# Spreading B, C and the time step over the partitions: transfers through DRAM in place of products with ones and zeros

## The chip, the core and the metric

The kernel runs on one core of one Trainium2 chip. Its engines work side by side, each through its own list of instructions in order: TensorE (PE, products; its weight loads are listed as PEld), VectorE (DVE), ScalarE (ACT), GpSimd (POOL) and SyncE (SP), which here only issues transfers. An engine waits for another through semaphores. The metric is the device time in microseconds (us), as the median of several executions.

## The reference

One layer for 8 sequences ("batches") of 512 steps and 512 channels: a layer norm, a selective scan (Mamba) on 1024 inner channels with 16 states each, a gated feed-forward network whose gate is modulated by an attention, and `x + s * silu(g)`. What the change touches is the part of the scan that comes from a projection on 33 columns:

```python
p = x_conv @ W_x.T                       # 33 columns
Bm, Cm = p[..., :16], p[..., 16:32]
dt = softplus(p[..., -1] + mean(dt_bias))
A = -exp(A_log)
def step(h, inp):
    x_t, B_t, C_t, dt_t = inp
    h = exp(A * dt_t) * h + dt_t * B_t * x_t
    y_t = einsum('bds,bs->bd', h, C_t)
```

All of it is in 32-bit floats.

## The kernel before

**Two stages.** The attention of all batches comes first (to about 760 us of the span), and writes its results to DRAM. Then a long loop goes over 8 batches x 64 scan steps. A scan step holds 8 channels x 16 states on the 128 partitions, for two groups of channels, with the 512 time steps along a row. Scan step k is split in two "chunks", one for each group. For each group ACT makes the decay `exp(A dt)` (line 549), DVE runs the scan instruction (569); the input is multiplied by dt B on DVE or POOL in turn (561, 563), and the result by C on POOL (574). After four scan steps PE sums over the states with a 0/1 matrix (`y`, 586), three scan steps later than the last of the four.

**What runs in the gaps.** All large products are cut into parts of about four matmuls, in one list for each batch (`batch_parts`): the gate and up products of the feed-forward net (293), its down products (`down_proj`, 355), the output products of the batch before (384), the input products and convolutions of the batch after (201, `conv_in`), the z gates, and the step sizes of the batch after (`step_size`). The main loop runs parts in proportion to the scan steps done. A part returns follow-up work with a delay in chunks: `(1, copies)` runs one chunk after the part. So the order on each engine is written out by the program, and no engine reorders it.

**Loads.** `prefetch` looks up to eight parts ahead and loads weights, in SP's queue: at most three quarters of a down product are ahead of the one in use (four buffers, `wd`). The scan inputs `x` are loaded five scan steps ahead (`load_scan`, eleven buffers), each 512 KB, repeated over 16 partitions. SP issues in program order; a load that has to wait for its buffer holds all behind it.

**B, C and dt before.** For batch b+1, `step_size` works during batch b's down products, in five parts placed between quarters of the products for m = 0, 1, 2. `project` makes the 33 rows `p`, in two halves (rows 0 to 32 and 64 to 96) that ACT copies to `parts_p`. `turned` turns the last row into a column with four small products; DVE and ACT compute softplus on 128 x 4. `step` spreads dt: DVE builds a diagonal `dg`, PE multiplies it by ones, ACT copies the result (`dt`). `output` and `input_` spread C and B with the 0/1 matrix `lift`, which also adds the two halves; ACT copies C (`cc`), DVE multiplies B by dt (`bb`). The scan of batch b+1 uses `dt` in its decays, `bb` in its inputs and `cc` in its outputs.

The attention stage has a spread through DRAM of its own: for batches 1 to 7 `statistics` writes 512 numbers to `scr_r` in the same turned way and reads them back as a row for all partitions (`rms`, lines 856 and 857).

Of the kernel before, what the change touches and what calls it, by code (L numbers as in the profile page):

```python
# [10 lines left out]
F32 = mybir.dt.float32  # L11
AF = mybir.ActivationFunctionType
ALU = mybir.AluOpType
# [4 lines left out]
P = 128  # L18
NB = 8
S = 512  # L20
DM = 512
KT = DM // P
TT = S // P
DI = 1024
ND = DI // P
NS = 16
# [13 lines left out]
def mamba_gated_ffn_kernel(  # L40
# [22 lines left out]
    nc = tc.nc  # L63

    const = ctx.enter_context(tc.tile_pool(name="const", bufs=1))
    dram = ctx.enter_context(tc.tile_pool(name="scratch", bufs=1, space=DRAM))

    scr_x = [dram.tile([P, 2 * KT, S], F32, tag=f"scr_x{b}", name=f"scr_x{b}") for b in range(NB)]
    scr_m = [dram.tile([R, S], F32, tag=f"scr_m{b}", name=f"scr_m{b}") for b in range(NB)]
    scr_c = [dram.tile([DI, S], F32, tag=f"scr_c{b}", name=f"scr_c{b}") for b in range(NB)]  # L70
    scr_r = [dram.tile([S], F32, tag=f"scr_r{b}", name=f"scr_r{b}") for b in range(NB)]
# [10 lines left out]
    act = ctx.enter_context(tc.tile_pool(name="act", bufs=2))  # L82
    xcp = ctx.enter_context(tc.tile_pool(name="xcp", bufs=2 * ND))
    tmc = ctx.enter_context(tc.tile_pool(name="tmc", bufs=2))
# [7 lines left out]
    def bank(name):  # L92
        if banks["special"]:
            return banks["special"](name)
        banks["n"] += 1
        pool = banks["second"] if banks["second"] and banks["n"] % 4 // 2 else ps_1
        return pool.tile([P, 512], F32, tag="mm", name=name)
# [3 lines left out]
    def load_xn(b):  # L101
        xnt[b] = act.tile([P, KT, S], F32, tag="xnt", name=f"xnt_{b}")
        nc.sync.dma_start(xnt[b], scr_x[b][:, :KT, :])

    def load_h(b):
        ht[b] = act.tile([P, KT, S], F32, tag="ht", name=f"ht_{b}", bufs=1)
        nc.sync.dma_start(ht[b], scr_x[b][:, KT:, :])
        modh[b] = act.tile([4 * QD, S], F32, tag="modh", name=f"modh_{b}", bufs=1)
        for i in range(4):
            nc.sync.dma_start(modh[b][i * QD : i * QD + R, :], scr_m[b])  # L110

    xc, gates, mlp, modh, spread, ys = {}, {}, {}, {}, {}, {}
# [14 lines left out]
    parts_p = wp.tile([P, S], F32, tag="parts_p", name="parts_p")  # L127
# [293 lines left out]
    def step_size(b):  # L421

        st = {}
        W = 2 * NS + 1

        def project():

            ps = bank(f"ps_p_{b}")
            for d in range(ND):
                at = 64 * (d % 2)  # L430
                nc.tensor.matmul(  # L431
                    ps[at : at + W, :], lhsT=wx[:, d, :], rhs=xc[b, d], start=(d < 2),
                    stop=(d >= ND - 2),
                )

            def copies():
                for at in (0, 64):
                    nc.scalar.copy(parts_p[at : at + W, :], ps[at : at + W, :])
                st["parts"] = parts_p

            return [(1, copies)]

        def lifted(i, name):
            ps = bank(f"ps_{name}_{b}")
            nc.tensor.matmul(ps, lhsT=lift[:, i, :], rhs=parts_p, start=True, stop=True)
            return ps

        def turned():

            ps = bank(f"ps_v_{b}")  # L450
            for tt in range(TT):
                nc.tensor.matmul(
                    ps[:, tt : tt + 1], lhsT=st["parts"][:, ts(tt, P)], rhs=lift[:, 2, 0:1],
                    start=True, stop=True,
                )
            st["v"] = ps[:, :TT]
            return [(1, exponential), (2, logarithm), (3, softplus)]

        def exponential():
            s = tmc.tile([P, 5, TT], F32, tag="sp", name=f"sp_{b}")
            st["sp"] = v, ee, ww, ln, dd = [s[:, i, :] for i in range(5)]
            nc.vector.tensor_scalar(v, st["v"], mb, None, ALU.add)
            nc.scalar.activation(ww, v, AF.Abs)
            nc.scalar.activation(ee, ww, AF.Exp, scale=-1.0)

        def logarithm():
            v, ee, ww, ln, dd = st["sp"]
            nc.vector.tensor_scalar(ww, ee, 1.0, None, ALU.add)  # L470
            nc.scalar.activation(ln, ww, AF.Ln)
            nc.vector.tensor_scalar(dd, ww, 1.0, None, ALU.subtract)
            nc.vector.tensor_scalar(ww, dd, 0.0, None, ALU.is_equal)
            nc.vector.tensor_tensor(dd, dd, ww, ALU.add)
            nc.vector.reciprocal(dd, dd)
            nc.vector.tensor_tensor(dd, dd, ee, ALU.mult)

        def softplus():
            v, ee, ww, ln, dd = st["sp"]
            nc.vector.tensor_tensor(ln, ln, ww, ALU.add)  # L480
            nc.vector.tensor_tensor(ln, ln, dd, ALU.mult)
            nc.vector.scalar_tensor_tensor(dd, v, 0.0, ln, ALU.max, ALU.add)
            dg = tmc.tile([P, TT, P], F32, tag="conv", name=f"dg_{b}")
            nc.vector.tensor_tensor(
                dg, ident.unsqueeze(1).to_broadcast([P, TT, P]),
                dd.unsqueeze(2).to_broadcast([P, TT, P]), ALU.mult,
            )
            st["dg"] = dg

        def step():  # L490
            ps = bank(f"ps_dt_{b}")
            nc.tensor.matmul(
                ps, lhsT=ones, rhs=st["dg"].rearrange("p t c -> p (t c)"), start=True, stop=True
            )
            st["sd"] = act.tile([P, S], F32, tag="dt", name=f"dt_{b}")
            nc.scalar.copy(st["sd"], ps)
            return []

        def output():
            ps = lifted(1, "cc")  # L500
            sc = act.tile([P, S], F32, tag="cc", name=f"cc_{b}")
            nc.scalar.copy(sc, ps)
            st["sc"] = sc
            return []

        def input_():
            ps = lifted(0, "bb")
            sb = act.tile([P, S], F32, tag="bb", name=f"bb_{b}")

            def scaled():  # L510
                nc.vector.tensor_tensor(sb, ps, st["sd"], ALU.mult)
                spread[b] = (sb, st["sc"], st["sd"])

            return [(1, scaled)]

        return (
            [(4, [], project)], [(1, [], turned)], [(1, [], step)], [(1, [], output)],
            [(1, [], input_)],
        )

# [80 lines left out]
    def batch_parts(b):  # L601

        quads = [gate_up(b, fq) for fq in range(NF // 4)]
        sizes = ([], [], [], [], [])
        parts = quads[0][0] + quads[0][1]
        if 0 < b < NB - 1:
            parts.insert(1, (0, [], lambda: load_xn(b + 1)))
        convs = [[]] * ND
        if b + 1 < NB:
            convs = [conv_in(b + 1, d) for d in range(ND)]  # L610
            sizes = step_size(b + 1)
        if b > 0:
            done = [finish(b - 1, m) for m in range(KT)]
            parts += done[0][0] + done[1][0] + [done[0][1]] + done[2][0] + [done[1][1]]
            parts += convs[0] + done[3][0] + [done[2][1]] + convs[1]
            turns = [done[3][1]]
        else:
            parts += convs[0] + convs[1]
            turns = []
        parts += quads[1][0] + turns + convs[2] + quads[1][1] + convs[3] + convs[4]  # L620
        parts += quads[2][0] + convs[5] + quads[2][1] + convs[6]
        parts += quads[3][0] + convs[7] + quads[3][1]
        for m in range(KT):
            down = down_proj(b, m)
            if m == 0:
                parts += down[:2] + sizes[0] + down[2:3] + sizes[1] + down[3:]
            elif m == 1:
                parts += down + sizes[2]
            elif m == 2:
                parts += down[:1] + sizes[3] + down[1:2] + sizes[4] + down[2:]  # L630
            else:
                parts += down
            if m == 0 and b + 1 < NB:
                parts.append((0, [], lambda: load_h(b + 1)))
        total = sum(p[0] for p in parts) + 4 * ND
        done, out_, z = 0, [], 0
        for p in parts:
            while z < ND and done >= total * (8 * z + 5) / STEPS and not p[3:]:
                out_ += z_gate(b, z)
                done += 4  # L640
                z += 1
            out_.append(p)
            done += p[0]
        while z < ND:
            out_ += z_gate(b, z)
            z += 1
        return out_
# [38 lines left out]
    with ExitStack() as c1:  # L686
# [423 lines left out]
        sizes = step_size(0)  # L1110
# [34 lines left out]
        for g in range(len(items)):  # L1145
# [3 lines left out]
            b, hg = cur  # L1149
# [18 lines left out]
            convs = g - (len(items) - 5)  # L1168
# [13 lines left out]
            for s in range(TT):  # L1182
                for w in ORDER[s]:
# [23 lines left out]
                    elif todo[w]:  # L1207
                        f = todo[w].pop(0)
# [70 lines left out]
    for b in range(NB):  # L1279
# [3 lines left out]
        for s in range(STEPS):  # L1283
            k = b * STEPS + s
            if s == STEPS - 6 and b + 1 < NB:

                parts = batch_parts(b + 1)
# [100 lines left out]
```

## Time and profile before

| | |
|---|---|
| median of 3 runs | 3105.28 us (3104.54 to 3106.17) |
| the profiled execution | 3103.03 us, its span 3101.2 us |
| granted TensorE clock, mean | 0.995 |
| attention stage, 0 to 760 us: PE busy | 715.66 us |
| 1330 to 1530 us: PE, DVE, ACT, POOL busy | 200.00, 176.00, 78.84, 155.59 us |
| transfers in that stretch | 209 GB/s, DMA share 0.78 |
| bytes moved in all | 505.10 MB |

The span is the time from the first to the last instruction of one execution that the hardware profiler recorded; the execution's own time is a little more. "Busy" counts the time in which an engine works on at least one instruction. A row of the timeline has the start, the length, the engine, the line of the kernel, the operation, the tile written and the tiles read, the shape and the number of instructions; in brackets stands how long the engine had been idle before and which instruction ended that. The waits of SP are those of its transfers' issues, not of the transfers.

### The profile page before, as it was taken

What the parts mean: (1) busy time and instruction counts of PE and PEld (TensorE: products, weight loads), DVE (VectorE), ACT (ScalarE), POOL (GpSimd) and SP (SyncE); (2) the same over time, 40 slices, a digit from 0 to 9 for tenths busy, and PEclk for the clock granted to TensorE, in tenths of its full rate; (3) what the DMA queues carried; (4) which work ended last, traced back from release to release, by engine and by line L of the source; (5) the groups of instructions that cost most, each with busy time, mean ns of one, the idle gap of its engine ahead of it and who ended that gap; (6) DMA issues with size and microseconds to landing.
All of it is one profiled execution on the core that took longest, in us unless ns stands there. A gap on an engine that the chain in (4) does not pass through costs nothing.

```text
span 3101.2 us, 34502 instructions
## 1 busy us (share of the span) xinstructions
PE 3046.4 (98%) x11740; PEld 1358.7 (44%) x11740; DVE 2611.0 (84%) x3393; ACT 1332.3 (43%) x2248; POOL 1902.8 (61%) x876
## 2 busy tenths in 40 slices
PE   8999999988999999999999999999999999999999
PEld 4555555544433444444344434444444444444443
DVE  6888888865999889879987988898889878988885
ACT  4555656544444334433443433344334433443332
POOL 3111111100788877777777777777777777778884
PEclk9999999999999999999999999999999999999999
DMA  3111111111977787678677867877787778777874
GB/s 115 46 46 46 45 45 46 59 46 47 236 209 190 193 226 203 181 200 218 187 200 200 225 175 206 216 203 183 193 227 193 191 191 224 201 187 187 218 198 114
DMA packets 295263, 505.10 MB, mean 163 GB/s; under 512 B 30352, under 2 KB 161936, under 8 KB 290480
## 3 DMA queue, kind: packets, MB, share of 16 engines
q1 hardware_dynamic: 293680, 494.25, 59.9%
q0 software_dynamic: 1408, 8.65, 0.7%
q8 instruction: 94, 1.54, 0.2%
q14 instruction: 81, 0.66, 0.1%
HBM read 460.53 MB, written 42.29 MB: 162 GB/s over the span
## 4 chain that ended last, share of the span: by engine, by line
PE 92%; DVE 5%; issue 1%; DMA 1%; ACT 1%; POOL 0%; SPq 0%; POOLq 0%; ACTq 0%; DVEq 0%
PE ps_gu L293 28%; PE ps_acc L355 14%; PE ps_in L201 14%; PE y L586 8%; PE ps_out L384 7%; PE ps_pt L1012 4%; PE ps_k L966 3%; PE ps_q L966 3%; PE s L981 3%; PE o_ps L1026 2%; PE ps_z L948 2%; PE ps_gu L304 1%; DVE x L569 1%; PE ps_p L431 1%; DVE mx L991 1%
## 5 line engine op out<-in xcount | busy, mean ns | idle before, releaser
L574 POOL TENSOR_TENSOR x<-x,cc 128x1024 f32<-128x1024 f32 x512 | 1203.9, 2361 | 500.5 <-DVE x L569 471.4
L569 DVE TENSOR_TENSOR_SCAN x<-decay,x 128x512 f32<-128x512 f32 x1024 | 1206.4, 1209 | 31.2 <-ACT decay L549 31.2
L549 ACT ACTIVATE decay<-dt,an 128x511 f32<-128x511 f32 x1024 | 695.8, 687 | 653.9 <-DVE x L569 649.2
L293 PE MATMUL ps_gu<-ht,wgu 128*128 128x512 f32 x2048 | 910.8, 597 | 0.8 <-DVE mod_t L1063 0.8
L293 PEld LDWEIGHTS ps_gu<-ht,wgu 128*128 128x128 f32 x2048 | 381.4, 190 | 517.9 <-issue 473.6
L563 POOL TENSOR_TENSOR x<-x,bb 128x1024 f32<-128x1024 f32 x256 | 605.0, 2363 | 4.2 <-DMA x<-scr_c 4.2
L201 PE MATMUL ps_in<-xnt,win 128*128 128x512 f32 x1024 | 459.8, 595 | 1.2 <-DVE m L323 1.2
L355 PE MATMUL ps_acc<-m,wd 128*128 128x512 f32 x1024 | 453.9, 596 | 0.0
L1064 POOL DMA_DIRECT2D scr_m<-mod_t x8 | 4.0, 498 | 577.1 <-DVE mod_t L1063 505.9
L561 DVE TENSOR_TENSOR x<-x,dtb_ps 128x1024 f32<-128x1024 f32 x256 | 306.2, 1196 | 3.7 <-DMA x<-scr_c 2.6
L355 PEld LDWEIGHTS ps_acc<-m,wd 128*128 128x128 f32 x1024 | 191.2, 190 | 253.8 <-issue 247.3
L201 PEld LDWEIGHTS ps_in<-xnt,win 128*128 128x128 f32 x1024 | 191.0, 190 | 244.7 <-issue 222.8
L997 ACT ACTIVATE p<-s,mx 128x384 f32<-128x384 f32 (+3 forms) x512 | 238.0, 525 | 133.5 <-DVE mx L991 129.9
L586 PE MATMUL y<-x,sel 128*32 128x512 f32 x2048 | 252.9, 601 | 3.7 <-POOL x L574 3.6
L384 PE MATMUL ps_out<-xc,wout 128*128 128x512 f32 x512 | 225.9, 594 | 0.0
L991 DVE TENSOR_REDUCE mx<-s 128x2 f32<-128x256 f32 (+3 forms) x256 | 211.1, 825 | 8.8
L240 DVE SCALAR_TENSOR_TENSOR conv<-ps_in,cw,conv 128x511 f32<-128x511 f32 (+2 forms) x192 | 143.5, 747 | 66.1 <-ACT conv L259 61.5
L1012 PE MATMUL ps_pt<-ident,p 128*128 128x128 f32 x1280 | 181.7, 279 | 12.6 <-DVE xc L250 5.8
L1012 PEld LDWEIGHTS ps_pt<-ident,p 128*128 128x128 f32 x1280 | 141.8, 141 | 92.8 <-issue 46.1
L384 PEld LDWEIGHTS ps_out<-xc,wout 128*128 128x128 f32 x512 | 95.8, 190 | 121.4 <-issue 121.4
L1017 DVE COPY pt<-ps_pt 128x512 f32<-128x512 f32 x191 | 123.3, 682 | 26.0 <-PE ps_pt L1012 25.1
L987 DVE TENSOR_TENSOR s<-s,mask 128x256 f32<-128x256 f32 x256 | 109.1, 426 | 36.9 <-PE s L981 36.0
(182 smaller groups left out, 2244.8 us busy)
## 6 DMA issues: line engine op xcount, KB each, us to landing
x<-scr_c SPq DMA_DIRECT2D x512, 512.0 KB
wgu<-in_w_ffn SPq DMA_DIRECT2D x256, 256.0 KB
win<-in_w_in SPq DMA_DIRECT2D x128, 256.0 KB
wd<-in_w_ffn SPq DMA_DIRECT2D x128, 256.0 KB
scr_c<-xc SPq DMA_DIRECT2D x64, 256.0 KB
wout<-in_out_w SPq DMA_DIRECT2D x64, 256.0 KB
xt<-in_x SPq DMA_DIRECT2D x32, 256.0 KB
scr_x<-xnT SPq DMA_DIRECT2D x8, 1024.0 KB
```

What stands on the lines that cost most here:

```text
L201: nc.tensor.matmul(ps, lhsT=w[:, kt, :], rhs=xnt[b][:, kt, :], start=(kt == 0), stop=(kt == KT - 1))
L293: nc.tensor.matmul(st[i, which], lhsT=w[:, kt, :], rhs=ht[b][:, kt, :], start=(kt == 0), stop=(kt == KT - 1 and (which == 1 or i == 3)),)
L355: nc.tensor.matmul(st["acc"], lhsT=w[:, j, :], rhs=mlp[b, f], start=(f == 0), stop=(f == NF - 1))
L384: nc.tensor.matmul(st["ps"], lhsT=w[:, d % 4, :], rhs=xc[b, d], start=(d == 0), stop=(d == ND - 1),)
L549: nc.scalar.activation(decay[n][:, 1:], spread[b][2][:, 1:], AF.Exp, scale=an[:, g // 4, g % 4 : g % 4 + 1])
L561: nc.vector.tensor_tensor(t, t, dtb_ps.unsqueeze(1).to_broadcast([P, 2, S]), ALU.mult)
L563: nc.gpsimd.tensor_tensor(t, t, spread[b][0].unsqueeze(1).to_broadcast([P, 2, S]), ALU.mult)
L569: nc.vector.tensor_tensor_scan(t, decay[n], t, 0.0, ALU.mult, ALU.add)
L574: nc.gpsimd.tensor_tensor(t, t, spread[b][1].unsqueeze(1).to_broadcast([P, 2, S]), ALU.mult)
L586: nc.tensor.matmul(y[ts(j, QD), :], lhsT=sel[:, i0 + n, :], rhs=xs[k - 3 + j][:, n, :], start=(i0 + n == 0), stop=(i0 + n == 3),)
L991: nc.vector.reduce_max(mx[i], sc[i][:, :, :w], axis=AX.X, negate=True)
L1012: nc.tensor.transpose(ps[:, ts(h, P)], probs[b, hg, qt][:, h, ts(kt, P)], ident)
```

## The change

For the first batch nothing changes, except that its steps are described by the same functions. For the other seven, `project` is the only part left on PE. ACT copies the upper half of `p`, DVE adds the lower one to it, and SP writes the 33 rows to a new tile in DRAM, `scr_p`. Two chunks later SP reads the last row back as a column (`v`) and B and C as rows, each repeated on 8 partitions. Softplus is as before, at chunks 7 to 9 after the part; its result goes to the last row of `scr_p` as single elements, and two chunks on (`rows`, 11) comes back as a row for all 128 partitions. At chunk 14 DVE multiplies B by dt. In `batch_parts` the five places for step sizes become one: ahead of all down products, after the last gate and up products; convolution 7 moves up by one place so that `project` has all it needs.

```diff
+    scr_p = [
+        dram.tile([2 * NS + 1, S], F32, tag=f"scr_p{b}", name=f"scr_p{b}") for b in range(NB)
+    ]
...
-            return [(1, copies)]
+            if b == 0:
+                return [(1, copies)]
+
+
+            def copy():
+                nc.scalar.copy(parts_p[64 : 64 + W, :], ps[64 : 64 + W, :])
+
+            def add():
+                nc.vector.tensor_tensor(parts_p[:W, :], ps[:W, :], parts_p[64 : 64 + W, :], ALU.add)
+
+            def send():
+                nc.sync.dma_start(scr_p[b], parts_p[:W, :])
+
+            def spread_out():
+                st["v"] = tmc.tile([P, TT], F32, tag="v", name=f"v_{b}", bufs=1)
+                nc.sync.dma_start(st["v"], scr_p[b][2 * NS].rearrange("(t p) -> p t", p=P))
+                st["sc"] = act.tile([P, S], F32, tag="cc", name=f"cc_{b}")
+                st["sb"] = act.tile([P, S], F32, tag="bb", name=f"bb_{b}")
+                for i, t in enumerate((st["sb"], st["sc"])):
+                    r = scr_p[b][i * NS : (i + 1) * NS, :]
+                    nc.sync.dma_start(t, r.unsqueeze(1).to_broadcast([NS, P // NS, S]))
+
+            return [
+                (1, copy), (2, add), (2, send), (4, spread_out), (7, exponential), (8, logarithm),
+                (9, softplus),
+                (11, rows), (14, scaled),
+            ]
...
             nc.vector.scalar_tensor_tensor(dd, v, 0.0, ln, ALU.max, ALU.add)
+            if b:
+                nc.sync.dma_start(scr_p[b][2 * NS].rearrange("(t p) -> p t", p=P), dd)
+                return
...
+        def rows():
+            st["sd"] = act.tile([P, S], F32, tag="dt", name=f"dt_{b}")
+            nc.sync.dma_start(st["sd"], scr_p[b][2 * NS].partition_broadcast(P))
+
+        def scaled():
+            nc.vector.tensor_tensor(st["sb"], st["sb"], st["sd"], ALU.mult)
+            spread[b] = (st["sb"], st["sc"], st["sd"])
...
+        if b:
+            return ([(4, [], project)],)
...
-        sizes = ([], [], [], [], [])
+        sizes = ([],)
...
-        parts += quads[2][0] + convs[5] + quads[2][1] + convs[6]
-        parts += quads[3][0] + convs[7] + quads[3][1]
+        parts += quads[2][0] + convs[5] + quads[2][1] + convs[6] + convs[7]
+        parts += quads[3][0] + quads[3][1] + sizes[0]
         for m in range(KT):
             down = down_proj(b, m)
-            if m == 0:
-                parts += down[:2] + sizes[0] + down[2:3] + sizes[1] + down[3:]
-            elif m == 1:
-                parts += down + sizes[2]
-            elif m == 2:
-                parts += down[:1] + sizes[3] + down[1:2] + sizes[4] + down[2:]
-            else:
-                parts += down
+            parts += down
             if m == 0 and b + 1 < NB:
                 parts.append((0, [], lambda: load_h(b + 1)))
```

More of the change, by code (lines that the diff above doesn't have):

```diff
@@ L508, in input_, with multiplied @@
             sb = act.tile([P, S], F32, tag="bb", name=f"bb_{b}")
-            def scaled():
+            def multiplied():
                 nc.vector.tensor_tensor(sb, ps, st["sd"], ALU.mult)
                 spread[b] = (sb, st["sc"], st["sd"])
-            return [(1, scaled)]
+            return [(1, multiplied)]
+        if b:
+            return ([(4, [], project)],)
         return (
```

## The prediction

> **What bounds the kernel now.** I read the page's busy shares first, then busy time by stage, then the order of work round one batch's step sizes, then who waits on whom.
>
> ```profile
> PE 3046.4 (98%) x11740; PEld 1358.7 (44%) x11740; DVE 2611.0 (84%) x3393; ACT 1332.3 (43%) x2248; POOL 1902.8 (61%) x876
> ```
>
> TensorE is busy for all but 2% of the span. By stage (stretch, its length, then PE, PEld, DVE, ACT, POOL busy, granted clock, DMA share, GB/s) it is sharper:
>
> ```profile
> 950.00:1030.00 80.00, 76.44 (x241) 29.90 (x234) 71.42 (x77) 33.53 (x52) 66.72 (x30) 0.98 0.75 190
> 1030.00:1250.00 220.00, 220.00 (x681) 90.02 (x680) 193.21 (x210) 87.12 (x137) 169.24 (x73) 1.00 0.78 207
> 1530.00:1630.00 100.00, 100.00 (x304) 41.00 (x303) 81.83 (x90) 39.00 (x61) 74.56 (x33) 1.00 0.71 188
> ```
>
> After the first batch of the scan PE never stops: batches repeat every 294.0 us (`ps_p` starts at 1559.0, 1853.1, 2147.1, 2441.1 and 2735.2). What leaves PE there is gained in full, and what makes PE wait there is lost in full. DVE, 82 to 88% busy in these rows, has slack but feeds PE: scan (DVE), then product with C (POOL), then `y` (PE).
>
> **What goes from PE.** One batch's steps on PE (start, length, instructions; a logical 512-column product is two instructions):
>
> ```profile
> 1559.04 3.63 PE L431 MATMUL ps_p<-xc,wx 128*33 128x512 f32 x16
> ...
> 1568.08 1.05 PE L452 MATMUL ps_v<-lift,parts_p 128*128 128x1 f32 x8
> 1568.99 10.55 PE L355 MATMUL ps_acc<-m,wd 128*128 128x512 f32 x24
> ...
> 1591.73 1.02 PE L492 MATMUL ps_dt<-dg,ones 128*128 128x512 f32 x2
> 1592.59 3.60 PE L355 MATMUL ps_acc<-m,wd 128*128 128x512 f32 x8
> 1596.02 1.02 PE L445 MATMUL ps_cc<-parts_p,lift 128*128 128x512 f32 x2
> 1596.88 3.60 PE L355 MATMUL ps_acc<-m,wd 128*128 128x512 f32 x8
> 1600.31 1.02 PE L445 MATMUL ps_bb<-parts_p,lift 128*128 128x512 f32 x2
> 1601.26 1.92 PE L586 MATMUL y<-x,sel 128*32 128x512 f32 x16
> ```
>
> From each start to the next: `ps_v` 0.91, `ps_dt` 0.86, `ps_cc` 0.86, `ps_bb` 0.95: 3.58 us a batch, on the engine that sets the end. Seven batches: **-25 us**. `ps_p` (3.55) stays.
>
> **What else moves, at nothing.** ACT loses three copies a batch (0.58 + 0.58 + 0.59); at 43% busy it is not the bound. DVE swaps the `dg` product (0.69) for the addition of the two halves of `ps_p` (as the nearest row, `bb` from PSUM, 0.69). The wait of DVE and ACT for `ps_p` stays, since the one copy left still waits for it. The bank of `ps_p` is held a chunk longer, which four banks cover; four fewer banks per batch leave their rotation as it was. New traffic is about 0.84 MB a batch, against 200 GB/s times 294 us = 59 MB: 1.4%, under a DMA share of 0.7 to 0.8. conv 7 moves ahead of the last gate products, on the same engines.
>
> **What is added: a chain through SP's queue.** SP issues in order and its loads wait for PE to free buffers, so it stands about where PE stands. I lay the changed order of batch 4 (2 to 7 are alike) on PE's own durations: T = 0 where `ps_p` starts, 3.43 for a quarter `d` of a down product, 3.52 for a z product, 1.86 for a burst of `y`. PE: `ps_p` to 3.6, d0.0 and d0.1 to 10.4, `y` to 12.3, d0.2 to d1.1 to 26.0, z to 29.5, `y` to 31.4, d1.2 to d2.1 to 45.1, then the `y` of the scan steps 244 to 247.
>
> 1. Copy (0.58) and addition end near T+5. SP has waited at `send` since before T; behind it stands d0.3's weight load, which PE needs at 15.7: hidden. `send` is whole 2 KB rows; it lands by about 8, then v, bb, cc are issued. They land by about 13 to 15, DVE wants v at 16.4 (242's scans, the `y` it waits for at 12.3, one product): no wait.
> 2. The softplus keeps its length:
>
> ```profile
> 1571.93 0.22 DVE L464 TENSOR_SCALAR sp<-ps_v,mb 128x4 f32<-128x4 f32 x1
> ...
> 1578.99 2.22 DVE L482 SCALAR_TENSOR_TENSOR sp<-sp 128x4 f32<-128x4 f32 x1
> ```
>
> 1571.93 to 1581.21 is 9.3, so the time step is ready at T+25.7. SP waits for it from about 16.7; behind it stand `ht`, `modh` and the loads of d1.3 (needed at 34.8) and d2.0 (38.2).
>
> 3. The time step is written to DRAM as 512 separate 4-byte elements and read back as a row for 128 partitions. The kernel has the same pair already, `scr_r` and `rms` in the attention stage:
>
> ```profile
> 496.30 0.38 SPq L856 DMA_DIRECT2D scr_r<-rs  x1
> 505.05 0.32 SPq L857 DMA_DIRECT2D rms<-scr_r  x1
> ```
> ```profile
> 511.07 1.27 POOL L939 TENSOR_TENSOR hT<-xnT,rms 128x512 f32<-128x512 f32 x1 [1.99 <-DMA rms<-scr_r]
> ```
>
> SP waited 8.75 us here for 2 KB to land, and 10.2 at 247.3; over the seven the mean is 9.1. From the read's issue to POOL's start: 4.1 to 6.5, mean 5.6. So dt lands at 25.8 + 9.1 + 0.5 (a weight issue between) + 5.6 + 0.8 (estimate: 256 KB of weights ahead of it, and the 1 MB of `ht`, which went out just before) = **T+41.8**.
>
> 4. DVE reaches `scaled` at about T+34 (eight rows after softplus, 1.13 a scan) and stands still for 8 us; every scan stands behind it. Then `scaled` and 246's second scan, POOL's product of 246 (2.36), its input product of 249 (2.36), its product of 247 (2.36): the `y` of 244 to 247 is ready 9.0 after dt, at T+50.8. PE wants it at 45.1. **PE waits 5.7 us.** Meanwhile d2.0 and d2.1 are loaded late too, since the order of the changed program lets SP issue d2.0 only after the element write has landed (it takes that write's semaphore, eight transfers on): d2.0 lands near 38.5 for 38.2, d2.1 behind 1.3 MB near 43.6 for 41.7. Both fit inside the same 5.7.
>
> Sum per batch: -3.6 + 5.7 = +2.1; seven batches +15. In the first stretch above PE already loses 3.56 us once, at batch 1's sizes; that wait is replaced, not added to: **+11 us**. The profiled run took 3103.03 (span 3101.2): 3114. The median of the runs is 2.25 above it: 3116.
>
> **A rule against the row.** The Trainium skill, "DMA: Bandwidth & Descriptors", section "Anatomy of one DMA — SWDGE (gpsimd) path", gives a transfer a fixed cost of about 2.0 us plus its bytes over 436 GB/s. By it 2 KB takes 2.0 and 256 KB 2.6, dt lands at 25.8 + 2.0 + 0.5 + 2.6 = T+31, before DVE asks, and the whole 25 us are kept: 3080. The same page ("Rules for kernel authors") warns that a last dimension that isn't contiguous becomes one descriptor per element, and ("Specifications") that under 512 B a transfer reads, modifies and writes; that speaks against this change, and the 8.75 us row is on its side. I take the row.
>
> **Bounds.** By the rows' ends (8.5 + 4.1, without the 0.8; 10.2 + 6.5 with it) PE waits 2.8 to 7.7 a batch; times seven, less 25 and less the 3.56 of batch 1, that is -9 to +25 us: 3096 to 3130. The rows come from a stage with DMA nearly idle; here it is at 0.7 to 1.06, so the upper end is nearer.
>
> **Rivals.**
> - *The transfers are hidden* (the rule's time, or DVE far enough ahead of PE): 3080, or up to 3099 where PE waits less than 3.2 a batch. For it: DVE waits for PE often (3.99 us at `ps_p`), so it has room. Against: the 8.75 us row, and only some 2 us between the unstalled `y` (T+43) and PE.
> - *Break-even*: PE waits 3.2 to 5.0 a batch, about what it is spared: 3099 to 3111. For it: the shorter rows give this. Against: they come from an idle DMA.
> - *SP's holds starve PE of weights*. Place: d1.3 and d2.0, with three quarters (10.3 us) of cover. SP stands 9 us at the softplus, then up to 9 for the write. From a landing of 12 us on, d2.0 lands near 42, then d2.1 behind the row and two 512 KB loads near 47, and the `y` near 54: a wait of 9, 9 x 7 - 25 - 3.6 = +34: 3139 or more. For it: 1 MB of `ht` sits in the same place. Against: loads there take 3 to 9 us in the trace and none stalled PE.
> - *It doesn't do what it says*: batch 0 keeps its products in either version; nothing else stays.
>
> **Chances.** Late time step with a wait of 5.0 to 8, 0.48; hidden, wholly or mostly, 0.25; break-even 0.15; starved weights 0.12. A change under 0.2% (6 us) can't be told from none. So faster 0.25, same 0.15, slower 0.60. Range 3080 to 3138, which takes in the hidden case and leaves out the starved one; the likeliest case alone is 3111 to 3132.
>
> **What would show it.** Right: PE busy falls by 25 us, yet gaps of 4 to 8 us appear on PE before a `y`, once a batch, some 45 us after `ps_p`, released by POOL; DVE idles at `scaled` for the dt row; SP waits about 9 us for the element write. Wrong: no such gaps and batches of 290.4 us (hidden), or gaps at L355's weights (starved). If the element write lands in 2 us here, or DVE comes to `scaled` later than T+40, the forecast fails to the fast side.

## The result, and the profile after

The changed kernel takes 3150.32 us (median of 4 runs, 3148.23 to 3151.93), the kernel before 3105.33: a ratio of 1.0147, 95% interval 1.0134 to 1.0159. It is slower by 45 us, four times the 11 us that were forecast and outside the range. The profiled execution has a span of 3149.5 us, against 3101.2.

The first row of the page shows TensorE with less work, in a longer span.

```profile
PE 3041.6 (97%) x11642; PEld 1350.9 (43%) x11642; DVE 2616.6 (83%) x3393; ACT 1320.1 (42%) x2227; POOL 1904.8 (60%) x876
```

PE is busy only 4.8 us less than before, although 98 instructions and 25 us of work are gone: where PE runs, it runs slower in places (below). Its idle time, span less busy time, has grown by 53.1 us, from 54.8 to 107.9. The page's rows for the down products, before and after (busy time, mean ns, idle time just before them), say where:

```profile
L355 PE MATMUL ps_acc<-m,wd 128*128 128x512 f32 x1024 | 453.9, 596 | 0.0
...
L358 PE MATMUL ps_acc<-m,wd 128*128 128x512 f32 x1024 | 469.0, 613 | 52.5 <-DMA wd<-in_w_ffn 52.5
```

Batches now repeat every 301 to 302 us (`ps_p` starts at 1262.3, 1563.8, 1865.1, 2167.4, 2468.2 and 2769.0) in place of 294.0.

Who waits for whom, in the changed kernel (us in total, times, longest):

```profile
DVE bb L527 <- DMA dt<-scr_p: 93.8, 7, 15.1
...
PEld ps_acc L358 <- DMA wd<-in_w_ffn: 63.7, 14, 8.9
...
PE ps_acc L358 <- DMA wd<-in_w_ffn: 52.5, 12, 8.1
...
PEld y L628 <- POOL x L616: 22.2, 23, 2.9
```

PE waits for the weights of the down products, which never held it in the kernel before. For `y` it waits no more than before (there 30.7 us, 36 times). DVE's wait for dt is long, 13.4 us a time, but it isn't what ends PE's waits: the 52.5 us for weights are all but the whole growth of PE's idle time.

One batch on PE, by time (start, length, instructions; in brackets the idle time before and what ended it); the first row is from the kernel before, two quarters at full speed:

```profile
1552.08 7.03 PE L355 MATMUL ps_acc<-m,wd 128*128 128x512 f32 x16
...
1865.11 3.63 PE L434 MATMUL ps_p<-xc,wx 128*33 128x512 f32 x16
...
1896.80 3.70 PE L358 MATMUL ps_acc<-m,wd 128*128 128x512 f32 x8
1908.31 9.71 PE L358 MATMUL ps_acc<-m,wd 128*128 128x512 f32 x16 [7.81 <-DMA wd<-in_w_ffn]
1918.90 3.70 PE L358 MATMUL ps_acc<-m,wd 128*128 128x512 f32 x8 [0.88 <-DMA wd<-in_w_ffn]
```

PE stands still at d1.3 for 7.8 us, then takes 9.7 for two quarters, which took 7.03 before, then waits once more, for d2.1. What happened to those weights is in SP's own queue:

```profile
1890.51 0.37 SPq L513 DMA_DIRECT2D scr_p<-sp  x1
1890.92 0.50 SPq L110 DMA_DIRECT2D ht<-scr_x  x1
1891.51 1.77 SPq L113 DMA_DIRECT2D modh<-scr_m  x4
1893.38 0.39 SPq L226 DMA_DIRECT2D wd<-in_w_ffn  x1
1893.87 0.53 SPq L583 DMA_DIRECT2D x<-scr_c  x1
1902.19 0.39 SPq L226 DMA_DIRECT2D wd<-in_w_ffn  x1
1905.43 0.34 SPq L524 DMA_DIRECT2D dt<-scr_p  x1
```

The element write goes out at 1890.51. The load for d1.3 is issued at 1893.38 and PE can use it at 1908.31, 14.9 us later. SP itself stands still too: it issues d2.0 only at 1902.19, when the write has landed, and the read of dt only at 1905.43, when `ht` has. Over the run:

```profile
SPq L226 <- DMA scr_p<-sp: 34.7, 6, 7.7
SPq L524 <- DMA ht<-scr_x: 27.4, 6, 5.9
```

And in the stretches of 2 us from there (the last three columns are granted clock, DMA share and GB/s):

```profile
1892.00:1894.00 2.00, 2.00 (x7) 0.80 (x6) 2.00 (x3) 1.33 (x2) 0.60 (x1) 1.00 2.56 66
1894.00:1896.00 2.00, 2.00 (x15) 0.60 (x17) 2.00 (x3) 1.00 (x3) 2.00 (x2) 1.00 0.51 33
1896.00:1898.00 2.00, 2.00 (x13) 0.68 (x4) 2.00 (x3) 0.99 (x2) 2.00 (x1) 1.00 1.07 33
1898.00:1900.00 2.00, 2.00 (x6) 0.76 (x4) 0.40 (x1) 0.69 (x1) 2.00 (x2) 1.00 0.66 25
1900.00:1902.00 2.00, 0.50 (x2) 0.00 (x0) 0.00 (x0) 0.00 (x0) 0.42 (x1) 1.00 0.28 25
1902.00:1904.00 2.00, 0.00 (x0) 0.00 (x0) 0.00 (x0) 0.00 (x0) 0.00 (x0) 0.82 0.82 297
1904.00:1906.00 2.00, 0.00 (x0) 0.00 (x0) 0.00 (x0) 0.00 (x0) 0.00 (x0) 0.50 1.06 273
...
1908.00:1910.00 2.00, 1.69 (x2) 0.84 (x3) 0.00 (x0) 0.00 (x0) 0.00 (x0) 0.50 1.15 198
```

For ten microseconds behind the write, with 1 MB of `ht` and more in the queue, the 16 DMA engines together move 25 to 66 GB/s, then at once 297. The DMA share is no help in seeing it here: it counts the time that packets took, and they took long. The bytes show it. At the end of the wait PE's granted clock is at 0.50, which is where the 9.71 us come from.

So the theory to test: **W**, the write of 512 single elements holds up the transfers behind it for some 10 us, and PE runs out of weights. Its rivals: **H**, SP standing at the softplus is enough, since it delays the same loads; **B**, the 1 MB of `ht` ahead of the weights is the cause; **D**, DVE's wait for dt is.

### The profile page after: what moved, and what is told of

It is laid out like the page before. It is cut to its first block, busy times and chain, and to the rows that moved or that the text cites. A ratio compares the mean times of both kernels' runs of the same rounds, so it can differ in the third digit from the quotient of the medians.

```text
span 3149.5 us, 34332 instructions
## 1 busy us (share of the span) xinstructions
PE 3041.6 (97%) x11642; PEld 1350.9 (43%) x11642; DVE 2616.6 (83%) x3393; ACT 1320.1 (42%) x2227; POOL 1904.8 (60%) x876
## 4 chain that ended last, share of the span: by engine, by line
PE 83%; DVE 7%; DMA 5%; issue 2%; POOL 2%; ACT 1%; SPq 0%; POOLq 0%; ACTq 0%; DVEq 0%
PE ps_gu L296 27%; PE ps_in L204 12%; PE ps_acc L358 9%; PE ps_out L387 7%; PE y L628 7%; PE ps_pt L1047 4%; PE ps_k L1001 3%; PE ps_q L1001 3%; PE s L1016 3%; PE o_ps L1061 2%; DMA wd<-in_w_ffn 2%; DMA ht<-scr_x 2%; PE ps_z L983 2%; DVE x L611 1%; POOL x L616 1%
## 5 line engine op out<-in xcount | busy, mean ns | idle before, releaser
L358 PE MATMUL ps_acc<-m,wd 128*128 128x512 f32 x1024 | 469.0, 613 | 52.5 <-DMA wd<-in_w_ffn 52.5
```

The costliest lines, as they stand in the source:

```text
L358: nc.tensor.matmul(st["acc"], lhsT=w[:, j, :], rhs=mlp[b, f], start=(f == 0), stop=(f == NF - 1))
```

## Experiments

Each was run beside the kernel before; that took 3103.97 with e1 to e4, 3105.29 with e5 to e8, 3103.2 with e9 to e11. e7 and e8 have four runs each, the others one.

### e1: no element write

```diff
-                nc.sync.dma_start(scr_p[b][2 * NS].rearrange("(t p) -> p t", p=P), dd)
                 return
...
-            nc.sync.dma_start(st["sd"], scr_p[b][2 * NS].partition_broadcast(P))
+            nc.sync.dma_start(st["sd"], scr_r[b].partition_broadcast(P))
```

> The element write is left out, and the row of dt comes from the 512 numbers that the attention stage left in DRAM (so dt is not the time step; B and C are as before). All else, the row's transfer at chunk 11 too, stays. Theory W (the write of 512 single elements holds up the 16 DMA rings for some 10 us, so that ht and the weights of d1.3 behind it come late and PE runs dry): no wait of PE for weights, batches of about 290.4 us, 3079 to 3086. Rival H (SP's hold at the softplus, and the order of its queue behind it): also gone here, since SP doesn't wait for softplus any more, 3079 to 3086. Rival B (1 MB of ht ahead of d1.3's weights): stays, some 3110 to 3150.

Measured: 3079.2 us. PE waits for weights once, 1.3 us, and `ps_p` starts at 1544.5, 1835.0 and 2125.5: batches of 290.5 us, 3.5 less than before. All that the change takes from PE is gained once the write is gone, though the row for dt, B, C and v still come through DRAM. `ht` stands ahead of the same weights here, but goes out 8 us earlier in the batch (1852.27), since SP isn't held; so against B this says little, and the next run decides.

### e2: SP held at softplus, 16 bytes in place of 512 elements

```diff
-                nc.sync.dma_start(scr_p[b][2 * NS].rearrange("(t p) -> p t", p=P), dd)
+                nc.sync.dma_start(scr_r[b].unsqueeze(0)[:, :TT], dd[0:1, :])
...
-            nc.sync.dma_start(st["sd"], scr_p[b][2 * NS].partition_broadcast(P))
+            nc.sync.dma_start(st["sd"], scr_r[b].partition_broadcast(P))
```

> In place of 512 elements the write sends 16 bytes, four results of softplus in one run, to the row that dt is then read from (dt is not the time step but for those four). SP is held at the softplus as in the changed kernel. Theory W: the write lands in about 2 us, DMA keeps 200 GB/s and more behind it, PE does not wait for d1.3; 3080 to 3092. Rival H: the hold alone starves PE, 3130 to 3155. Rival B: 3110 to 3150.

Measured: 3090.22 us. SP's queue and the DMA in this run, at the same place of a batch:

```profile
1866.28 0.25 SPq L513 DMA_DIRECT2D scr_r<-sp  x1
1866.58 0.35 SPq L110 DMA_DIRECT2D ht<-scr_x  x1
...
1872.10 0.34 SPq L524 DMA_DIRECT2D dt<-scr_r  x1
```
```profile
1868.00:1870.00 2.00, 2.00 (x6) 0.95 (x5) 2.00 (x2) 1.38 (x2) 0.82 (x1) 1.00 0.79 295
1870.00:1872.00 2.00, 2.00 (x14) 0.42 (x16) 2.00 (x3) 1.18 (x2) 2.00 (x2) 1.00 1.02 319
```

SP reaches softplus's result as late as in the changed kernel, `ht` follows as there, and the DMA moves 295 and 319 GB/s. dt is issued 5.8 us after the write, not 14.9. With 1 MB of `ht` ahead of the weights at the same place, B alone is out. H costs something: 11 us over e1, with PE waiting 4.7 us for weights over the whole run, and DVE 27.2 for dt. It is not the 45.

### e3: the element write from ACT's queue

```diff
-                nc.sync.dma_start(scr_p[b][2 * NS].rearrange("(t p) -> p t", p=P), dd)
+                nc.scalar.dma_start(scr_p[b][2 * NS].rearrange("(t p) -> p t", p=P), dd)
```

> The same element write, issued from ACT's queue; SP is no longer held at the softplus. Theory W, if the stall is of the 16 engines: 3130 to 3160, with ht and d1.3's weights still landing 10 us late. If the stall is of SP's own rings only: 3080 to 3100. Rival H: 3080 to 3095.

Measured: 3116.46 us, below the low end of the expectation, 3130. SP is free at the softplus, so `ht` goes out at 1868.44, 8 us ahead of the write (ACT, 1876.62), and PE doesn't wait for d1.3. But SP is held a little later all the same. After a weight load at 1877.80 it issues nothing until the read of dt, which waits for the write to land:

```profile
1877.80 0.39 SPq L226 DMA_DIRECT2D wd<-in_w_ffn  x1
1886.29 0.34 SPq L524 DMA_DIRECT2D dt<-scr_p  x1
...
1887.93 2.40 SPq L226 DMA_DIRECT2D wd<-in_w_ffn  x2
```
```profile
1878.00:1880.00 2.00, 2.00 (x6) 0.90 (x5) 2.00 (x3) 1.22 (x2) 0.49 (x1) 1.00 1.04 211
1880.00:1882.00 2.00, 2.00 (x15) 0.55 (x17) 2.00 (x3) 1.01 (x3) 2.00 (x2) 1.00 0.56 117
1882.00:1884.00 2.00, 2.00 (x15) 0.68 (x8) 2.00 (x3) 1.10 (x2) 2.00 (x1) 1.00 0.00 0
...
1888.00:1890.00 2.00, 2.00 (x6) 0.89 (x5) 0.00 (x0) 0.00 (x0) 0.00 (x0) 1.00 0.87 117
```

The six microseconds without a byte, 1882 to 1888, are those in which SP has issued nothing more; they are no stall of queued transfers. PE then waits 3.54 us, until 1897.01, for d2.1, which was issued at 1887.93, and 27.2 us in 9 such waits over the run. So this run shows the write's own latency again, 9.7 us from its issue to the read of dt, and what SP's order makes of it. Whether such a write holds up the transfers of another queue it doesn't settle. The only load issued after the write, at 1877.80, landed at 1886.4 by the trace's semaphore records, together with the write (1886.2); that is a hint, no more.

### e4: the kernel before, with the element write added

```diff
             nc.vector.scalar_tensor_tensor(dd, v, 0.0, ln, ALU.max, ALU.add)
+            if b:
+                nc.sync.dma_start(scr_p[b].rearrange("(t p) -> p t", p=P), dd)
```

> The kernel before, with the element write of the time step added after softplus (SP's queue, for batches 1 to 7; nothing reads it), PE's products stay. Theory W: DMA falls under 70 GB/s for some 8 to 10 us behind each write; the cover of the weights there is three quarters of a down product, so PE waits 0 to 6 us a batch: 3108 to 3147. Rivals H and B: no stall of the rings, 3104 to 3112.

Measured: 3126.95 us against 3103.97: +23.0, or 3.3 us for each of the seven writes, which nothing reads. In the batch at 1863.2 the write goes out at 1885.40, and then:

```profile
1885.00:1887.00 2.00, 2.00 (x5) 0.59 (x4) 1.97 (x3) 0.00 (x0) 0.36 (x1) 1.00 0.13 1
1887.00:1889.00 2.00, 2.00 (x18) 0.49 (x17) 2.00 (x3) 1.70 (x3) 0.57 (x1) 1.00 0.02 4
1889.00:1891.00 2.00, 2.00 (x5) 0.98 (x6) 2.00 (x3) 0.54 (x2) 2.00 (x2) 1.00 0.22 35
1891.00:1893.00 2.00, 2.00 (x6) 0.87 (x5) 2.00 (x3) 0.98 (x2) 2.00 (x1) 1.00 0.21 24
1893.00:1895.00 2.00, 2.00 (x6) 0.84 (x5) 2.00 (x3) 0.72 (x2) 2.00 (x2) 1.00 0.22 29
1895.00:1897.00 2.00, 1.92 (x5) 0.57 (x3) 1.55 (x3) 0.18 (x1) 2.00 (x2) 1.00 0.13 18
1897.00:1899.00 2.00, 0.00 (x0) 0.00 (x0) 2.00 (x3) 2.00 (x4) 0.73 (x1) 1.00 0.95 249
```

1 to 35 GB/s for 12 us, PE empty at its end. The weights that went out right behind the write reach PE 13.3 us later:

```profile
1885.40 0.38 SPq L485 DMA_DIRECT2D scr_p<-sp  x1
1885.87 0.46 SPq L224 DMA_DIRECT2D wd<-in_w_ffn  x1
```
```profile
1899.18 3.67 PE L356 MATMUL ps_acc<-m,wd 128*128 128x512 f32 x8 [2.26 <-DMA wd<-in_w_ffn]
```

This is W by itself: no step of the change but the write, to a tile of its own.

### e5: ht two down products later

```diff
-            if m == 0 and b + 1 < NB:
+            if m == 2 and b + 1 < NB:
                 parts.append((0, [], lambda: load_h(b + 1)))
```

> The changed kernel with the loads of ht and modh for the next batch put after the down product m = 2 instead of m = 0. Theory W (the element write holds up whatever stands behind it): the weights of d1.3 and d2.0 are still behind the write, though no longer behind 1 MB too, so PE waits less, and dt still comes 15 us and more after softplus: 3110 to 3140. Rival B (ht ahead of the weights is the cause): 3080 to 3092.

Measured: 3124.62 us; PE waits 3.12 and 0.98 us in the batch at 1856.3, where the changed kernel waits 7.81 and 0.88. B has a share: with 1 MB less behind the write, 26 us of the loss go. But `ht` costs only behind the write; in e2 it stands ahead of the same weights, at the same time, at little cost.

### e6: the same 2 KB in runs of 16 bytes

```diff
-                nc.sync.dma_start(scr_p[b][2 * NS].rearrange("(t p) -> p t", p=P), dd)
+                nc.sync.dma_start(scr_p[b][2 * NS].rearrange("(p t) -> p t", p=P), dd)
```

> The same 2 KB of results written as 128 runs of 16 bytes, one from each partition, in place of 512 runs of 4 (the row that comes back is in another order of time, so dt, and what follows from it, is another). If the stall goes with the number of pieces, it is about a quarter, 2 to 3 us: 3088 to 3105. If any transfer of such short pieces to DRAM stalls alike, 3135 to 3152.

Measured: 3097.45 us. dt is issued 7.5 us after the write (1866.74 and 1874.20), and the DMA is back at 291 GB/s from 1870. A quarter of the pieces, still side by side, and most of the stall gone; it fits a cost by piece, which e10 then refutes.

### e7: softplus on rows

```diff
-                st["v"] = tmc.tile([P, TT], F32, tag="v", name=f"v_{b}", bufs=1)
-                nc.sync.dma_start(st["v"], scr_p[b][2 * NS].rearrange("(t p) -> p t", p=P))
+                st["sd"] = act.tile([P, S], F32, tag="dt", name=f"dt_{b}")
+                nc.sync.dma_start(st["sd"], scr_p[b][2 * NS].partition_broadcast(P))
...
+        def row_exp():
+            st["e"] = tmc.tile([P, S], F32, tag="conv", name=f"e_{b}")
+            nc.scalar.activation(st["e"], st["sd"], AF.Abs, bias=mb)
+            nc.scalar.activation(st["e"], st["e"], AF.Exp, scale=-1.0)
+
+        def row_log():
+            nc.scalar.activation(st["e"], st["e"], AF.Ln, bias=1.0)
+
+        def row_sum():
+            nc.vector.tensor_scalar(st["sd"], st["sd"], mb, 0.0, ALU.add, ALU.max)
+            nc.vector.tensor_tensor(st["sd"], st["sd"], st["e"], ALU.add)
```

(The three run at chunks 7, 8 and 9, and `scaled` at 10; the column `v`, the element write and `rows` go. Softplus here leaves out the correction of the logarithm for small arguments.)

> Softplus without the turn: the last row of p is read from DRAM as a row for all partitions, together with B and C, and softplus is taken there, on 128 x 512 (ACT: abs, exp, log; DVE: two instructions; without the correction of the logarithm for small arguments that the 128 x 4 form has). No element write, no read of single elements, no hold of SP at softplus. Theory W: all of PE's 3.58 us a batch is kept, 3076 to 3083. A rival in which the spread through DRAM itself, its row transfers or its order in SP's queue, is what costs: 3095 or more.

Measured: 3077.54 us (3076.34 to 3079.45), 0.9912 of the kernel before, interval 0.9898 to 0.9927. Batches take 290.5 us and PE waits for no weights:

```profile
1330.00:1530.00 200.00, 200.00 (x623) 81.75 (x622) 178.46 (x196) 79.54 (x125) 153.49 (x67) 1.00 0.77 209
```

Of the versions here that compute the time step it is the fastest.

### e8: B and C through DRAM, the time step by the product with ones

```diff
-            if b:
-                nc.sync.dma_start(scr_p[b][2 * NS].rearrange("(t p) -> p t", p=P), dd)
-                return
...
-            return ([(4, [], project)],)
+            return ([(4, [], project)], [(1, [], step)])
...
-            parts += down
+            parts += down + (sizes[1] if m == 1 else [])
```

(The element write and `rows` go; `scaled` follows `step` by two chunks.)

> B, C and the column for softplus through DRAM as in the changed kernel, the time step spread by the diagonal product and ones as before (one part on PE after the second down product). PE keeps 2.72 us of the 3.58 a batch, 19 us in all. Theory W: 3082 to 3092, since nothing is written in single elements. Rival (reading single elements or the rows costs too): 3100 or more.

Measured: 3085.75 us (3085.32 to 3087.77), 0.9938, interval 0.9921 to 0.9954. Less 20 us, as the sum of `ps_v`, `ps_cc` and `ps_bb` says (2.72 x 7 = 19). The read of 512 single elements (v) is in it and costs nothing that shows.

### e9, e10, e11: where the elements go

All three read dt's row from `scr_r`, so that no one waits for the write's result. e9 changes nothing else and writes the elements side by side; e10 and e11 write them to a tile of their own, 64 and 512 bytes apart (G stands for 16 and 128).

```diff
+    scr_w = [dram.tile([S, G], F32, tag=f"scr_w{b}", name=f"scr_w{b}") for b in range(NB)]
...
-                nc.sync.dma_start(scr_p[b][2 * NS].rearrange("(t p) -> p t", p=P), dd)
+                nc.sync.dma_start(scr_w[b][:, 0].rearrange("(t p) -> p t", p=P), dd)
...
-            nc.sync.dma_start(st["sd"], scr_p[b][2 * NS].partition_broadcast(P))
+            nc.sync.dma_start(st["sd"], scr_r[b].partition_broadcast(P))
```

> The changed kernel with its element write, but the row of dt is read from the 512 numbers that the attention stage left (dt is not the time step), so that nothing waits for the write to land but the transfers behind it. Theory W: the weights alone carry the loss, 3130 to 3150, with DMA under 70 GB/s for some 10 us behind each write. Rival D (the loss comes from DVE's 15 us wait for dt): 3085 to 3105.

> As the run before, with the 512 elements written 64 bytes apart, each to a place of its own, instead of side by side. If it is the neighbours in one block of memory that hold each other up, the stall shrinks: 3080 to 3100. If every piece of 4 bytes costs its time wherever it goes, the same as dense within 8 us.

> As before, 512 bytes apart. If neighbours within 512 bytes hold each other up, only this one is fast, 3080 to 3100; if neighbours within 64 bytes do, both are; if pieces cost whatever their place, all three are alike within 8 us.

Measured: 3158.78, 3094.09 and 3095.98 us. e9 is slower still than the changed kernel, by 8 us in one run and above its expectation, for a reason that stays open. DVE there waits as long, for a row that was ready in DRAM since the attention stage, since its transfer stands in the same stalled queue. So D is not a cause but a mark of the same one. e10 has the same 512 pieces of 4 bytes as e9, from the same tile, at the same place of the program. From the write to the load of d2.0, first e9, then e10:

```profile
1894.25 0.37 SPq L513 DMA_DIRECT2D scr_p<-sp  x1
...
1906.24 0.39 SPq L226 DMA_DIRECT2D wd<-in_w_ffn  x1
```
```profile
1870.01 0.37 SPq L514 DMA_DIRECT2D scr_w<-sp  x1
...
1874.03 0.54 SPq L227 DMA_DIRECT2D wd<-in_w_ffn  x1
```

And the DMA in the second stretch of either:

```profile
1896.00:1898.00 2.00, 2.00 (x6) 0.95 (x5) 2.00 (x2) 1.37 (x2) 0.86 (x1) 1.00 1.36 25
```
```profile
1872.00:1874.00 2.00, 2.00 (x6) 0.76 (x4) 2.00 (x3) 1.13 (x2) 1.10 (x1) 1.00 0.85 242
```

242 GB/s two microseconds after the write, where e9 has 42, 25, 29, 37, 20 and 25 in six such stretches. By the traces' semaphore records the seven writes land 9.7 to 11.9 us after their issue in e9, and 1.9 to 2.4 in e10 and e11. The other tile isn't the reason, since e4 writes to a tile of its own too and stalls. So the number of pieces doesn't stall the DMA; that single elements lie side by side does. Neighbours alone don't do it either: in e6 runs of 16 bytes lie side by side, and land in 1.4 to 3.3 us. At which spacing below 64 bytes, or which length of a run below 16, the stall begins, and why it holds the DMA up so long, these runs don't show. What e10 still takes over e1, 15 us, is near e2's 11; SP's hold at softplus is in both.

## Why the prediction was wrong

- **What bounds the kernel, and what PE is spared**: right. e1 and e7 have batches of 290.5 us for the 290.4 that 294.0 - 3.58 gives, and lie 25 and 28 us under the kernel before.
- **The order of events up to softplus**: right to within 0.7 us. With T at 1865.1, softplus's result goes out at T+25.4 (25.7 in the sum), DVE reaches `scaled` at T+33.3 (34).
- **Step 3, the price of the element write**: this failed. The row of 8.75 us was nearly right as far as it goes: by the semaphore records the seven writes landed 9.3 to 11.6 us after their issue, 9.1 in the sum. It rightly beat the 2 us of the Trainium skill ("DMA: Bandwidth & Descriptors", "Anatomy of one DMA — SWDGE (gpsimd) path"), which would have given 3080; e10's elements, 64 bytes apart, do land in about that time (1.9 to 2.2). But I used the row as the latency of that one transfer. In the attention stage nothing stood behind it, so the row couldn't show what it does to others. Here the DMA was held for some 10 us, and `ht`, for which the sum had an estimate of 0.8 us, went through only after that. The read of dt was issued at T+40.3 in place of T+35.4, 2.2 us of it because the write landed later and 2.7 because the read waited for `ht` to land, which the sum didn't have. dt was ready at T+48.4 (1913.46), not T+41.8.
- **Step 4, what PE waits for**: this failed with it. The forecast was 5.7 us before a `y`, with the weights of d2.0 and d2.1 inside it. Measured were 7.81 and 0.88 before weights, the first at d1.3, a load that the sum held to be covered, and 2.7 more at half clock: 11.4 in this batch. Less 3.58 that is 7.8, and the batches are 6.8 to 8.3 longer. The last of the rivals, starved weights at 3139 or more, had the place, d1.3, and the price, from "a landing of 12 us on" (this batch's write landed after 11.6); it had a chance of 0.12 because loads at that place had never taken more than 9 us. That SP issues d2.0 only after the write has landed was forecast rightly.
- **The direction**: slower, as forecast, but by luck. The loss came through a wait that the sum held to be covered, and not through the late `y`.
- **Costs set at nothing**: the copies, the addition and the row transfers of B and C cost nothing (e8 keeps the sum). SP's hold at softplus was held to be covered; e2 puts it at up to 11 us in all, together with dt's late row.

## What to carry to other kernels

Before a transfer is priced at its own latency, ask what is queued behind it: a write of single elements side by side can hold up all that stands behind it in its queue, and in a kernel whose weights arrive just in time that is PE's time. Read GB/s beside the DMA share to find such a stretch. A column that has to become a row is better never made: softplus on 128 equal rows costs three ACT and two DVE instructions that other work hides, and spares both turns (e7).

## What the hardware showed that I had not expected

- 2 KB written to DRAM as 512 single elements side by side take 9.3 to 11.6 us to land (changed kernel), and hold the DMA behind them in the same queue at 25 to 66 GB/s for 10 us, or at 1 to 35 for 12 us (e4). The same elements 64 bytes apart do not (e10: 242 GB/s, landed in 1.9 to 2.2 us). The read of 512 such elements showed no cost (e8).
- The PE's granted clock fell from 1.00 to 0.50 2.8 us into the wait shown, and was still 0.62 in the stretch 1912 to 1914; two quarters of a down product took 9.71 us in place of 7.03. A wait of 7.8 us on PE thus cost 10.5. Over the seven waits of this size or near it (3.35 to 8.06 us) the clock fell 2.1 to 4.8 us after PE stopped, and came back 2.9 to 5.6 us after it went on; e3's wait of 3.54 us left it at 1.00. The Trainium skill, "TensorE: Matmul & The Clock Gate", section "What's actually happening", says that the clock goes to half after at least one idle window of about 3.4 us and comes back after at least one such window of work; both measured ranges lie round that figure.
